# An alignment directive ahead of the first query projection of each repeating pair of an attention kernel

## The chip, the cores and the metric

The kernel runs on one core of one Trainium2 chip. The metric is the device time of one launch in microseconds, as the median of several runs. The core's engines are TensorE (PE in the profile, with its weight loads apart as PEld), VectorE (DVE), ScalarE (ACT), GpSimd (POOL) and SyncE (SP), which issues most of the DMAs. Each engine has an instruction stream of its own, which a sequencer works through in order; engines wait for each other with semaphores.

## What is computed

Cross attention of 4 x 2048 rows with 16 heads of 32 against 77 keys per batch, with an output projection, a residual and a layer norm:

```python
def reference(x, ctx_1024, mask_BxSxS2_bk1, wq, wk, wv, wo, gamma, beta):   # names shortened
    # x (4, 2048, 512), ctx_1024 (4, 77, 512); B, S, D, H = (2, 1024, 512, 16), HD = 32, EPS = 1e-05
    qs = (q @ wq).reshape(Bq, Lq, H, HD).transpose(0, 2, 1, 3)
    ks_ = (k @ wk).reshape(Bq, Lk, H, HD).transpose(0, 2, 1, 3)
    vs = (v @ wv).reshape(Bq, Lk, H, HD).transpose(0, 2, 1, 3)
    scores = jnp.einsum('bhqd,bhkd->bhqk', qs, ks_) / jnp.sqrt(jnp.float32(HD))
    scores = jnp.where(mask[:, None, :, :], -jnp.inf, scores)
    attn_w = jax.nn.softmax(scores, axis=-1)
    attn = jnp.einsum('bhqk,bhkd->bhqd', attn_w, vs)
    attn = attn.transpose(0, 2, 1, 3).reshape(Bq, Lq, H * HD)
    out = attn @ wo + q
    mu = jnp.mean(out, axis=-1, keepdims=True)
    var = jnp.mean((out - mu) ** 2, axis=-1, keepdims=True)
    return (out - mu) / jnp.sqrt(var + EPS) * gamma + beta
```

Here q is x, k and v are the context, and all of it is float32.

## The kernel before

The 8192 query rows are cut into 64 tiles of 128 rows. Two tiles make a pair, and two pairs make a group of 512 rows, for which the queries are projected together. The large projections (queries, keys, values, output) split each float32 operand into a high and a low part and add three products, high by high, high by low and low by high; scores and attention times values are plain float32, of which each matmul of the program becomes two in the instruction stream.

Three pairs of tiles and the set-up are written out at the start. After them the function `pair(n)` runs for n from 3 (`JOIN // 2`) to 26 (`CUT - 1`), and an order written out by hand (`ORDER`) ends the program. Nothing is scheduled by a planner: the order of instructions on each engine is the order of the words of the string `PAIR`, which `pair(n)` reads word for word. A word's letter names a step and its number the tile, pair or query part relative to the present one. The words that put work on TensorE are, in this order:

- `S`: the score visit, first part. `scores_pair` writes the scores of both tiles into six banks of PSUM (sc and the shared sc_e and sc_f); 96 matmuls of 32 x 64 tiles in the stream.
- `D`: `scores_rest`, the other 32 of the visit's 128.
- `O-6` and `O-5`: `o_proj`, the output projections of two earlier tiles (po), 12 matmuls each.
- `Q5` and `Q6`: `q_visit`, two query parts of a later group (pq); one has 12 matmuls, the other 13.
- `V-2`: `av`, attention times values of an earlier pair (pa), 32 matmuls in the stream.

Every matmul is preceded in the stream by a load of its weights. A matmul or a weight load carries one semaphore to wait for; where more are needed, instructions that do nothing but wait stand ahead of it. They show in the profile as EVENT_SEMAPHORE on the sequencer of the weight loads (PEldq).

The eight banks of PSUM go round (`bank`). VectorE takes the maxima of the scores out of them (`maxima`, L364) and copies the queries (`q_evac`, L209); ScalarE takes the high part of attention times values (`av_hi`, AH) and VectorE the low part (`av_lo`, L512, AL), which the output projection multiplies. So the sequencer of TensorE waits for VectorE wherever a bank is to be used again. The instruction streams themselves are fetched by DMAs on queues of their own: the profile lists 55 packets and 0.90 MB on the queue of TensorE's, 16 KB a packet, which is a block of 256 of its some 14,100 instructions.

Of the kernel before, what the change touches and what calls it, by code (L numbers as in the profile page):

```python
# [40 lines left out]
JOIN = 6  # L41
# [35 lines left out]
def xattn_layernorm(  # L77
# [15 lines left out]
    nc = tc.nc  # L93
# [198 lines left out]
    def load_mask(b):  # L292
        m8 = sb.tile([P, TPB, NK2], U8, tag="m8", bufs=1, name=f"m8_{b}")
        nc.sync.dma_start(m8, mask[b])
        mb = sb.tile([P, TPB, NK2], BF16, tag="mb", name=f"mb_{b}")
        bat[b] = (mb, m8)
# [5 lines left out]
    def mask_quarter(b, i):  # L302
        mb, m8 = bat[b]
        ts = slice(i * TPB // 4, (i + 1) * TPB // 4)
        nc.vector.tensor_tensor(mb[:, ts], m8[:, ts], mcol.to_broadcast((P, TPB // 4, NK2)), ALU.mult)
# [23 lines left out]
    def scores_pair(b):  # L329
        for t in (2 * b, 2 * b + 1):  # L330
            nmax[t] = sb.tile([P, H], F32, tag="nm", bufs=3, name=f"nm_{t}")
            sums[t] = sb.tile([P, H], F32, tag="sum", bufs=3, name=f"sum_{t}")
            scs[t] = {}
        own = [bank(f"sc_{b}_{j}") for j in range(GH)]
        both = [bank(f"sc_{b}_{j}") for j in ("e", "f")]
        units = []
        for j in range(GH):
            mine = [(2 * b, g) for g in range(NG)] + [(2 * b + 1, g) for g in range(NG)]
            for i, (t, g) in enumerate(mine):
                bk, at = (own[j], i) if i < 6 else (both[j // 2], 2 * (j % 2) + i - 6)  # L340
                scs[t][g, j] = bk[:, at * NK : (at + 1) * NK]
            units.append(mine[6:] + mine[:6] if j % 2 == 0 else mine)
        for i in range(6):
            for half in range(0, P, P // 2):
                for j in range(GH):
                    score(*units[j][i], j, half, P // 2)
        held[b] = units

    def scores_rest(b):
        units = held.pop(b)  # L350
        for i in (6, 7):
            for js in ((0, 2), (3, 1)):
                for half in range(0, P, P // 2):
                    for j in js:
                        score(*units[j][i], j, half, P // 2)
# [71 lines left out]
    def regroup(b):  # L427
        for n in range(12):
            regroup_part(b, n, nc.sync)
# [323 lines left out]
    for u in range(0, JOIN, 2):  # L753
        n = u // 2
        m, k = divmod(u, TPB)
# [123 lines left out]
    def do(op, k, part=0, queue="s"):  # L879
        if op == "k" and k >= LATE:  # L880
            scale_one(k)
        elif op == "z" and k == NT - 1:
            finish_last(k)
        elif op == "w" and k == NT - 1:
            od.pop(k)
        elif op in tile_ops:
            tile_ops[op](k)
        elif op in tile_parts:
            lo, size = (q4 * part, q4) if part < 10 else (2 * part - 20, 2) if part < 20 else (part - 20, 1)
            tile_parts[op](k, lo, lo + size)  # L890
        elif op == "s":
            (moments_one if k >= LATE else moments)(k)
        elif op in "hm":
            (recip_half if op == "h" else normalise_half)(k, part)
        elif op in visits:
            visits[op](*divmod(k, 4))
        elif op in inputs:
            inputs[op](k // 2, k % 2 * 2)
        elif op == "P":
            regroup_part(k, part, by[queue])  # L900
        elif op == "U":
            regroup_tile(k, part, by[queue])
        elif op == "R":
            flip(k, part)
        elif op == "E":
            flip_evac(k, part, nc.vector.tensor_copy if queue == "v" else nc.scalar.copy)
        elif op == "Y":
            turn_values()
        elif op == "V":
            av(k)  # L910
        elif op in "ab":
            (av_hi if op == "a" else av_lo)(k, part)
        else:
            (av_hi if op == "c" else av_lo)(k // 2, k % 2, True)

    def read(word):
        op, (k, part) = word[0], (word[1:] + ".").split(".")[:2]
        queue = part[-1:] if part[-1:].isalpha() else ""
        return op, int(k or 0), int(part[: len(part) - len(queue)] or 0), queue or "s"

    def pair(n):
        u = 2 * n
        words = PAIR.split()
        if n == JOIN // 2:
            words.remove("O-6")
            words.insert(words.index("D"), "O-6")
        for word in words:
            op, k, part, queue = read(word)
            if op == "S":
                scores_pair(n)  # L930
            elif op == "D":
                scores_rest(n)
            elif op in "LB":
                m, at = divmod(u, TPB)
                if m + 1 < NB and op == "L" and at == TPB - 10:
                    load_mask(m + 1)
                elif m + 1 < NB and op == "B" and at >= TPB - 8:
                    mask_quarter(m + 1, (at - TPB + 8) // 2)
            elif op == "P" and "." not in word:
                regroup(n + k)  # L940
            elif op in "Qq":
                if op == "Q" or divmod(2 * n + k, 4) in qp:
                    do(op, 2 * n + k)
            elif op in "gij":
                do(op, n + k)
            elif op in "PVab":
                if op in "PV" or n + k > JOIN // 2 - 3:
                    do(op, n + k, part, queue)
            elif u + k >= 0:
                do(op, u + k, part, queue)  # L950

    for n in range(JOIN // 2, CUT):
        pair(n)
# [51 lines left out]
```

## Time and profile before

| What | Value |
|---|---|
| median of 3 runs | 506.88 us (506.75 to 507.35) |
| span of the profiled execution | 505.2 us; its own time is not listed apart from the span |
| TensorE matmuls, weight loads | 496.4 us (98%), 391.0 us (77%), 6908 of each |
| VectorE, ScalarE, GpSimd | 463.3 us (92%), 472.2 us (93%), 427.0 us (85%) |
| granted TensorE clock | 0.998 of full speed |
| DMA | 109.50 MB, mean 217 GB/s |
| TensorE's share of the chain that ended last | 90% |

The page of the profile lists busy times, the chain of work that ended last (followed back from the last instruction to what released each step) and the costliest groups. In rows of instructions the first number is the start in microseconds from the span's start, the second the duration, then engine, line, operation, output<-inputs and form.

### The profile page before, as it was taken

The numbers are of one execution on the slowest core, as the hardware profiler recorded it, in microseconds if no ns is written. First come the engines' busy times: TensorE is split into PE (matmuls) and PEld (weight loads), VectorE is DVE, ScalarE is ACT, GpSimd is POOL, SyncE is SP. The second block draws the span as 40 slices with busy tenths as digits, with TensorE's granted clock in tenths as the row PEclk, the third lists the DMA queues.
The fourth block names the chain that finished last, engine by engine and source line by source line (L and its number), as shares of the span: only waits on it lengthen the run. The fifth ranks groups of instructions, "written<-read, shape, count | busy, mean of one in ns | idle before, by whom it ended". The sixth has DMA issues, their size and how long they took to land.

```text
span 505.2 us, 20438 instructions
## 1 busy us (share of the span) xinstructions
PE 496.4 (98%) x6908; PEld 391.0 (77%) x6908; DVE 463.3 (92%) x2566; ACT 472.2 (93%) x2239; POOL 427.0 (85%) x384
## 2 busy tenths in 40 slices
PE   9999999999999999999999999999999999999994
PEld 7987778777777887777788777777877777777784
DVE  6698999999989998999999988999999889999997
ACT  6798999999999999999999999999999999999861
POOL 0659368989888998988999888889988888999994
PEclk9999999999999999999999999999999999999999
DMA  8945887677778779777878878787777878667665
GB/s 308 399 165 151 207 215 194 197 191 210 213 226 227 217 211 257 188 205 227 224 218 220 237 182 248 210 228 212 228 200 204 237 214 245 171 189 209 168 210 209
DMA packets 58280, 109.50 MB, mean 217 GB/s; under 512 B 9203, under 2 KB 10739, under 8 KB 58176
## 3 DMA queue, kind: packets, MB, share of 16 engines
q1 hardware_dynamic: 55776, 103.35, 72.5%
q0 software_dynamic: 1872, 4.20, 2.7%
q8 instruction: 55, 0.90, 0.8%
q10 hardware_dynamic: 528, 0.66, 0.4%
q14 instruction: 49, 0.40, 0.2%
HBM read 41.68 MB, written 16.78 MB: 116 GB/s over the span
## 4 chain that ended last, share of the span: by engine, by line
PE 90%; ACT 4%; DVE 3%; DMA 2%; issue 1%; SPq 1%; DVEq 0%; ACTq 0%
PE pq L192 31%; PE po L557 29%; PE pa L459 11%; PE sc L321 7%; PE sc L557 3%; ACT pbuf L379 3%; PE sc_e L321 2%; PE pv L258 2%; PE pk L218 1%; PE pq L709 1%; PE pq L190 1%; DMA PT<-B 1%; PE sc_f L321 1%; DMA xtf<-xT 1%; DVE pbuf L364 1%
## 5 line engine op out<-in xcount | busy, mean ns | idle before, releaser
L379 ACT ACTIVATE pbuf<-pbuf,nm 128x77 f32<-128x77 f32 x1024 | 352.5, 349 | 8.5 <-DVE nm L364 7.5
L379 ACT ACTIVATION_READ_ACCUMULATOR pbuf<-pbuf,nm 128x1 f32 x1024 | 193.5, 189 | 0.0
L390 POOL TENSOR_TENSOR pbuf<-pbuf,ri 128x1232 f32<-128x1232 f32 x63 | 145.9, 2317 | 19.7 <-DVE ri L385 15.7
L364 DVE CUSTOM_DVE_ANT_0 pbuf<-sc,mb 128x77 f32<-128x77 f32 x828 | 144.0, 232 | 5.9 <-PE sc L321 5.6
L192 PE MATMUL pq<-xtl,wqh 128*128 128x512 f32 (+1 forms) x256 | 98.3, 384 | 0.0
L192 PE MATMUL pq<-xth,wql 128*128 128x512 f32 (+1 forms) x256 | 98.2, 384 | 0.0
L413 DVE STREAM_TRANSPOSE B<-pbuf 128x1280 f32<-128x1280 f32 x63 | 94.6, 1503 | 0.4 <-POOL pbuf L390 0.2
L557 PE MATMUL po<-woh,AH 128*128 128x512 f32 x224 | 90.6, 405 | 0.0
L192 PE MATMUL pq<-xth,wqh 128*128 128x512 f32 (+1 forms) x230 | 88.6, 385 | 0.0
L557 PE MATMUL po<-wol,AH 128*128 128x512 f32 x224 | 87.4, 390 | 0.0
L585 POOL TENSOR_TENSOR o<-o,gam 128x512 f32<-128x512 f32 x53 | 68.7, 1297 | 21.0 <-ACT o L581 21.0
L557 PE MATMUL po<-woh,AL 128*128 128x512 f32 x224 | 86.5, 390 | 0.0
L364 DVE DVE_READ_ACCUMULATOR2_ANT nm<- 128x1 f32 x1024 | 84.7, 83 | 0.0
L586 POOL TENSOR_TENSOR o<-o,bet 128x512 f32<-128x512 f32 x53 | 68.4, 1290 | 4.2
L180 POOL TENSOR_TENSOR xtl<-xtf,xth 128x1024 fp32r<-128x1024 f32 x28 | 67.5, 2412 | 0.1
L459 PE MATMUL pa<-PT,vsb 96*32 96x256 f32 x960 | 58.2, 382 | 0.7 <-DMA PT<-B 0.3
L321 PE MATMUL sc<-kct,q 32*64 32x77 f32 x3312 | 55.2, 238 | 0.5 <-DVE q L209 0.5
L192 PEld LDWEIGHTS pq<-xth,wql 128*128 128x128 f32 x256 | 48.2, 188 | 8.4
L192 PEld LDWEIGHTS pq<-xtl,wqh 128*128 128x128 f32 x256 | 48.1, 188 | 8.5
L321 PEld LDWEIGHTS sc<-kct,q 32*64 32x64 f32 x3312 | 48.7, 130 | 6.5 <-issue 4.8
L557 PEld LDWEIGHTS po<-woh,AH 128*128 128x128 f32 x224 | 42.0, 188 | 10.8 <-DVE nm L364 0.4
L192 PEld LDWEIGHTS pq<-xth,wqh 128*128 128x128 f32 x230 | 43.2, 188 | 9.0
(176 smaller groups left out, 851.6 us busy)
## 6 DMA issues: line engine op xcount, KB each, us to landing
PT<-B SPq DMA_DIRECT2D x355, 128.0 KB
xtf<-xT SPq DMA_DIRECT2D x28, 512.0 KB
o<-x SPq DMA_DIRECT2D x56, 256.0 KB
out<-o SPq DMA_DIRECT2D x56, 256.0 KB
PT<-B POOLq DMA_DIRECT2D x16, 128.0 KB, 4.5
o_end<-x SPq DMA_DIRECT2D x7, 256.0 KB
out<-o_end SPq DMA_DIRECT2D x7, 256.0 KB
xtf<-xT SPq DMA_DIRECT2D x4, 256.0 KB
```

The costliest lines, as they stand in the source:

```text
L180: nc.gpsimd.tensor_tensor(l, fx.pop((g, c)), h.bitcast(F32), ALU.subtract)
L192: nc.tensor.matmul(pq, wc, r[:, c, rs], start=(n == 0), stop=(n == 11))
L258: nc.tensor.matmul(pv, ctx_s[c][i][:, r, :], v[c], start=(n == 0), stop=(n == 11))
L321: nc.tensor.matmul(scs[t][g, j][r0 : r0 + n], qd[t // 4][q, g, at : at + n], kct[q, g, t // TPB, keys_of(j)], start=True, stop=True,)
L364: nc.vector.tensor_tensor_reduce(pb[:, i // 2, (i % 2) * NK : (i % 2 + 1) * NK], scs[t][g, j], mb[:, t % TPB, keys_of(h)], -1.0, CEIL, ALU ...
L379: nc.scalar.activation(p, p, AF.Exp, bias=nmax[t][:, i : i + 1], scale=-1.0, accum_out=sums[t][:, i : i + 1])
L390: nc.gpsimd.tensor_tensor(pv, pv, rv.to_broadcast((P, NP, 2, NK)), ALU.mult)
L413: nc.vector.transpose(bt.rearrange("p c q r -> p q c r"), pbuf[t % NPB].rearrange("p q (c r) -> p q c r", c=5),)
L459: nc.tensor.matmul(pas[b, g // 2][HD * j : HD * (j + 1), (g % 2) * BLK : (g % 2 + 1) * BLK], vsb[:, 2 * b // TPB, HD * h : HD * (h + 1)], ...
L557: nc.tensor.matmul(pos[t][:, cols], a[:, c, rs], w[:, c, cols], start=go, stop=done)
L585: nc.gpsimd.tensor_tensor(o, o, gam, ALU.mult)
L586: nc.gpsimd.tensor_tensor(o, o, bet, ALU.add)
```

## The change

In `pair(n)`, for every n over 3, a call stands ahead of the word `Q5`:

```diff
             elif op in "Qq":
+                if op == "Q" and k == 5 and n > JOIN // 2:
+
+                    nc.tensor.addr_align(256, 40)
                 if op == "Q" or divmod(2 * n + k, 4) in qp:
                     do(op, 2 * n + k)
```

`addr_align(256, 40)` is a directive and no instruction of the engine. When the program is loaded it is replaced by as many instructions without effect, from 0 to 255, as are needed for the next instruction of TensorE to land in slot 40 of a block of 256; in the form used here (no bound on their number is given) the engine's sequencer executes them all. There are 23 of these directives, in the pairs 4 to 26. With 426 instructions from one directive to the next, the score visit of the following pair starts 121 slots after slot 40, at slot 161.

On TensorE at the end of the second output projection of pair 12 (po_19, from the attention rows' parts AH and AL and the weights' parts woh and wol; pq_7_1 is the query part that `Q5` stands for there, from the rows' parts xth and xtl), this stands before:

```order
L557 MATMUL po_19_3621<-woh_69,AH_9_3495 128x512
L557 MATMUL po_19_3621<-wol_70,AH_9_3495 128x512
L557 MATMUL po_19_3621<-woh_69,AL_9_3496 128x512
L192 MATMUL pq_7_1_3651<-xth_7_3045,wqh_67 128x512 [waits DVE_49,PE_49]
L192 MATMUL pq_7_1_3651<-xtl_7_3046,wqh_67 128x512
L192 MATMUL pq_7_1_3651<-xth_7_3045,wql_68 128x512
```

And this after:

```order
L557 MATMUL po_19_3629<-woh_69,AH_9_3503 128x512
L557 MATMUL po_19_3629<-wol_70,AH_9_3503 128x512
L557 MATMUL po_19_3629<-woh_69,AL_9_3504 128x512
L944 ISA
L192 MATMUL pq_7_1_3660<-xth_7_3051,wqh_67 128x512 [waits DVE_49,PE_49]
L192 MATMUL pq_7_1_3660<-xtl_7_3052,wqh_67 128x512
L192 MATMUL pq_7_1_3660<-xth_7_3051,wql_68 128x512
```

Only the directive (L944 ISA) is new, and it stands ahead of the query part's waits; no other instruction changes its place on any engine.

## The prediction

> **What bounds the kernel now.** I read the page first: span, busy times, chain.
>
> ```profile
> span 505.2 us, 20438 instructions
> PE 496.4 (98%) x6908; PEld 391.0 (77%) x6908; DVE 463.3 (92%) x2566; ACT 472.2 (93%) x2239; POOL 427.0 (85%) x384
> PE 90%; ACT 4%; DVE 3%; DMA 2%; issue 1%; SPq 1%; DVEq 0%; ACTq 0%
> ```
>
> TensorE carries 98% of the span and 90% of the chain that ended last, so a pair costs what TensorE spends on it. The other runs' median, 506.88, lies 1.7 us above this execution's span; I work in differences from 505.2 and add them to 506.88. Next, the chain in order of time, where each repeating pair shows as one output stretch (po, 24 matmuls), one query stretch (pq: 6 and 2 and 17), one attention-times-values stretch (pa, 32) and the score visit, which the view cuts into many short pieces:
>
> ```profile
> 91.84 5.66 PE po L557 x24
> 99.10 3.88 PE pq L192 x17
> 102.98 1.86 PE pa L459 x32
> 106.47 5.67 PE po L557 x24
> 121.28 5.67 PE po L557 x24
> 135.99 5.71 PE po L557 x24
> ...
> 341.65 5.66 PE po L557 x24
> 356.47 5.69 PE po L557 x24
> ...
> 400.54 5.67 PE po L557 x24
> ```
>
> The starts of po give a pair's period: first to last here is 308.70 us over 21 periods, 14.70 each; the shortest is 91.84 to 106.47, 14.63, the longest 341.65 to 356.47, 14.82. The fixed parts do not move (po 5.66 to 5.71, pq 3.88, pa 1.86), so nearly all of the spread of up to 0.19 us lies in the score visit, between pa and po. That is the whole prize: if each of the 23 pairs took the shortest period, 23 x 0.07 = 1.6 us.
>
> **What the change takes and adds.** A pair is 426 TensorE instructions: 24 + 25 + 32 + 128 matmuls, a weight load with each, and eight waits that stand alone (two at L192, four at L459, two at L321; rows below). Three pairs are 1278, two short of five blocks of 256, so today the block edge meets the score visit in three places in turn, shifting by only two slots every third pair. With the directive a pair must fill whole blocks: 512, so 512 - 426 = 86 padding instructions per pair, and the first query event sits at slot 40, the first score weight load 121 later, at 161. Nothing else is added, and no matmul, wait or DMA changes place; POOL's and SP's queues are not passed.
>
> *The padding's place.* It stands after the second output projection and ahead of the wait for the first query bank. What I must know is how long TensorE's sequencer is idle there, and how far it runs ahead of the array. One pair, from the windows of VectorE, of the weight loads and of L192, L459 and L321:
>
> ```profile
> 195.08 0.69 DVE L512 TENSOR_TENSOR AL<-pa,AH 128x512 fp32r<-128x512 f32 x1
> 198.21 0.24 DVE L364 CUSTOM_DVE_ANT_0 pbuf<-sc,mb 128x77 f32<-128x77 f32 x1
> 199.82 0.19 PEld L557 LDWEIGHTS po<-woh,AL 128*128 128x128 f32 x1
> 200.05 0.19 PEld L192 LDWEIGHTS pq<-xth,wqh 128*128 128x128 f32 x1
> L192 PEldq EVENT_SEMAPHORE  x2: 51/51/51, 198.5 to 200.2; - x2
> L459 PEldq EVENT_SEMAPHORE  x4: 51/51/51, 201.8 to 202.1; - x4
> L321 PEldq EVENT_SEMAPHORE  x2: 51/51/51, 191.7 to 191.9; - x2
> ```
>
> The ninth output matmul waits for the low half of the attention rows (AL), done at 195.08 + 0.69 = 195.77. After it nothing is left to wait for until the query event, which starts at 198.5, right after the VectorE maximum that frees its bank (198.21 + 0.24 = 198.45). So the sequencer stands at that event while the array still works off output matmuls, and the array wants the first query weights at 200.05. The 32 instructions in between cost little: the two L321 events, with 12 weight loads and matmuls between them, are 0.2 us apart, so I put 0.3 us. Window one, free of any effect: 198.45 - 195.77 - 0.3 = 2.4 us, or 28 ns for each of 86. Window two, until the array starves: 200.05 - 195.77 - 0.3, less 0.25 for the event and for the dispatch of the load, 3.7 us, or 43 ns each.
>
> *The price of one padding instruction* is in no row. Rows to bound it:
>
> ```profile
> 178.27 0.13 PEld L321 LDWEIGHTS sc_f<-kct,q 32*64 32x64 f32 x1
> 178.27 0.13 PEld L321 LDWEIGHTS sc<-kct,q 32*64 32x64 f32 x1
> 178.28 0.13 PEld L321 LDWEIGHTS sc_e<-kct,q 32*64 32x64 f32 x1
> 178.29 0.13 PEld L321 LDWEIGHTS sc<-kct,q 32*64 32x64 f32 x1
> ...
> 0.24 0.10 POOL L996 MEMSET const-float32-0.0<- 128x1 f32 x1 [0.24 <-issue]
> 0.27 0.10 POOL L996 MEMSET const-float32-1.0<- 128x1 f32 x1
> 0.30 0.10 POOL L996 MEMSET const-bfloat16-1.0<- 128x1 bf16 x1
> 0.33 0.10 POOL L996 MEMSET const-uint8-127<- 128x1 uint8 x1
> ```
>
> Below: weight loads of a score visit start some 7 ns apart, so 86 x 7 = 0.6 us. Above: the four L459 events follow each other by 0.3 / 3 = 0.1 us, so 86 x 0.1 = 8.6 us. In the middle: GpSimd's sequencer starts four small fills 30 ns apart, ordinary instructions without a wait. Padding has no semaphore either, and it isn't a matmul that goes straight to the array, so the fills are its nearest row: 86 x 30 = 2.6 us, 0.2 over window one and 1.1 inside window two. The query event then passes 0.2 us later, with the array still fed. I cost the padding at 0; its cover is the output projection's 24 matmuls, and if that cover ends (over 43 ns), the query projection is late next, once per pair.
>
> The Trainium skill, "DMA: Bandwidth & Descriptors", section "Anatomy of one DMA", puts an engine sequencer's dispatch at about 50 ns. By it the padding would be an estimated 4.3 us, 0.6 over the second window, and the 23 pairs would cost some 14 us. No row here shows a padding instruction, so it is not excluded.
>
> *The first padding* isn't 86: it depends on what the loader puts ahead of the program, which the trace doesn't show, and is 0 to 255. At 30 ns the middle, 128, is 3.8 us, 0.1 over the window; the worst is 7.7, so 4.0 once. I take +0.2.
>
> *The block edge.* Does its place matter? Sort the periods by their number in the sequence of three: by the 22 starts whose first and last rows stand above, the three groups average 14.67, 14.70 and 14.72 us. Scatter within a group (14.63 to 14.72, 14.63 to 14.81, 14.65 to 14.82) is larger than the distance between them. If every pair took the best group's mean, 23 x 0.03 = 0.7 us; if the worst's, a loss of 0.5. Counted from the program's first instruction the best group's visits begin near slot 155, close to the new 161; but the loader's own instructions ahead of the program shift that count by an unknown number, so 161 may fall to any group. I take 0.4 us of gain.
>
> *More blocks.* The page has the instruction fetch of TensorE on its own queue:
>
> ```profile
> q8 instruction: 55, 0.90, 0.8%
> ```
>
> 0.90 MB in 55 packets is 16 KB, 256 instructions of 64 B, each. The 22 later paddings add 22 x 86 / 256 = 7.4 blocks, with the first some 8: 63 packets, 0.1% more of the DMA engines. Hidden behind the 0.8% that is hidden today.
>
> The Trainium skill, "Runtime: NRT & Kernel Launch", section "Instruction fetch mechanics", speaks against the change: crossing a 16 KiB boundary is mostly hidden. By it the block-edge term is 0 and the sum +0.2. The trace agrees so far as the three groups differ by no more than 0.05 us.
>
> Sum: padding 0, first padding +0.2, block edge -0.4, fetch 0: -0.2, so 506.88 - 0.2 = 506.7.
>
> **Rivals.** (1) *Slower: padding at the price of an event on TensorE's queue.* It decides above 43 ns. An event is recorded as 51 ns: 86 x 51 = 4.4 us, 0.7 beyond the window, 23 x 0.7 = 16 us, 523. At 0.1 us a piece: 8.6 - 3.7 = 4.9, 113 us, 620. For it: the padding runs on the same sequencer as those events, whose follow-on time is more than three times that of GpSimd's fills. Against it: an event handles a semaphore, padding doesn't. The page's 50 ns, named above from the Trainium skill, leads into this rival. (2) *Faster: the block edge is what stretches the score visit, and 161 is a good place for it.* Then all pairs go to between the shortest period and the best group's mean, -0.7 to -1.6 us, 505.3 to 506.2; over 1.0 it can be measured. For it: two of the three groups are longer. Against: the scatter within them; a VectorE wait in the visit explains it as well. (3) *No change at all, or a change that isn't what it says:* if the loader adds nothing, or the edge has no price and padding none: 506.9, and the fetch packets tell which (55 or 63).
>
> **How the numbers follow.** A measurement of this kernel can tell about 0.2%, 1.0 us, from no change. Padding hidden and the edge worth less than 1.0 us, my forecast together with rival 3: 0.38, its own range 505.9 to 507.9. Rival 2 in its measurable part: 0.27, down to 505.2. Rival 1: 0.35, of which about half lies below 530 (53 ns, 10 ns over the limit: 86 x 10 x 23 = 20 us, and 3 for the first padding). So faster 0.27, same 0.38, slower 0.35, and the range 505.2 to 530 leaves out some 0.18, nearly all above.
>
> **What would show it.** Hidden: the first query weight load still follows the last output one by 0.23 us (199.82 to 200.05), the query event starts at most some 0.3 us later than the VectorE maximum before it, and periods stay at 14.63 to 14.82. Not hidden: an idle stretch of the weight loads ahead of L192 in every pair, put down to "issue". Edge right: periods all alike and near 14.65; edge worthless: as scattered as now. Fetch: 62 to 64 packets on the instruction queue. Wrong altogether: a padding price over 43 ns.

## The result, and the profile after

| | before | after |
|---|---|---|
| median of the runs on one chip | 507.1 us (506.4 to 507.6, 6 runs) | 588.06 us (582.72 to 591.47, 6 runs) |
| span of the profiled execution | 505.2 us | 586.8 us |
| granted TensorE clock | 0.998 | 0.964 |

The changed kernel is slower: the ratio to before is 1.158, with a 95% interval of 1.154 to 1.161. Every ratio, here and below, leaves out executions over 1.5% longer than the shortest of the same kernel (one of the six here, four of the six of e8, single ones of e1, e2 and e7), while the medians count them. The page, with the rows that answer to those of before (the last one is the fetch of TensorE's instructions):

```profile
span 586.8 us, 22437 instructions
PE 517.7 (88%) x6908; PEld 400.7 (68%) x6908; DVE 465.8 (79%) x2566; ACT 473.5 (81%) x2239; POOL 427.9 (73%) x384
PE 47%; DVE 44%; ACT 3%; issue 2%; DMA 2%; SPq 1%; DVEq 0%; ACTq 0%
q8 instruction: 63, 1.03, 0.8%
```

The span grew by 81.6 us while the work of VectorE, ScalarE and GpSimd stayed where it was (DVE 463.3 before, 465.8 now). There are 1999 instructions more, which the trace shows as 107 in the first padding and 22 x 86. TensorE's share of the chain fell from 90% to 47%, and VectorE's rose to 44%. That last row misleads, as the groups and the waits show. From the page's groups, the same line of before first, then of after, and then the waits of the weight loads after (total, times, longest):

```profile
L192 PE MATMUL pq<-xth,wqh 128*128 128x512 f32 (+1 forms) x230 | 88.6, 385 | 0.0
```

```profile
L192 PE MATMUL pq<-xth,wqh 128*128 128x512 f32 (+1 forms) x230 | 95.6, 416 | 59.4 <-DVE nm L364 52.0
```

```profile
PEld pq L192 <- issue: 68.5, 23, 4.3
```

The first query matmul of a pair now finds the array idle, 59.4 us in all where there was none. The group puts most of it to VectorE's maximum (nm L364), the last semaphore that the query event handles. The weight load in front of the same matmul, however, waits 68.5 us for "issue", 23 times, once per directive: nothing that the profile shows held it. That is TensorE's own sequencer, busy. One pair in the order of the instructions (the last output weight load, the padding of this pair in one row with its first and last start, the query events, the first query weight load):

```profile
212.52 0.19 PEld L557 LDWEIGHTS po<-woh,AL 128*128 128x128 f32 x1
215.48 0.19 PEld L192 LDWEIGHTS pq<-xth,wqh 128*128 128x128 f32 x1 [2.78 <-issue]
```

```profile
L944 PEldq NOP  x86: 13/13/13, 208.9 to 215.3; - x86
L192 PEldq EVENT_SEMAPHORE  x2: 51/51/51, 215.4 to 215.6; - x2
```

The 86 instructions without effect appear as NOP, each recorded as 13 ns, but their starts run from 208.9 to 215.3: 6.4 / 85 = 75 ns from one to the next. The sequencer reaches them while the array is still in the output projection, 0.45 us after VectorE has finished the low half of the attention rows (at 208.46 in this pair, and within 5 ns of that delay in all 22 later pairs), and it is done 2.78 us after the last output weight load has ended. Before, the query load followed the output load by 0.23 us.

The clock adds to it. The chain in order of time, for the same pair and the one ahead of it, and then three windows around the query stretch of this pair (busy times of PE, PEld, DVE, ACT and POOL, the granted clock, the DMA's share and GB/s):

```profile
198.23 1.62 PE pq L192 x6
200.09 3.88 PE pq L192 x17
...
215.51 1.65 PE pq L192 x6
217.59 5.25 PE pq L192 x17
```

```profile
213.50:217.00 3.50, 1.49 (x7) 1.26 (x8) 3.43 (x22) 3.50 (x22) 2.06 (x1) 1.00 0.58 164
217.00:220.40 3.40, 3.40 (x11) 2.72 (x10) 0.69 (x3) 2.76 (x13) 2.00 (x6) 0.50 0.89 204
220.40:224.00 3.60, 3.60 (x35) 2.49 (x37) 2.30 (x4) 0.10 (x1) 3.52 (x3) 1.00 0.86 226
```

In the pair at 198 the query stretch runs at the full clock and takes as long as before (3.88 for its 17). In the pair at 215 the granted clock is 0.50 from 217.0 to 220.4, and the stretch takes (217.59 - 215.51) - (200.09 - 198.23) + (5.25 - 3.88) = 1.6 us longer. The trace has 11 such stretches of 3.41 us among the pairs; before had none there.

Which pairs these are can be read from the trace. The starts of the stretches (87.27, 124.82, 141.88, 162.36, 216.98 us and so on) lie whole multiples of 3.413 us apart: 11, 5, 6 and 16 for these. If the time of the pairs is cut into windows of this length on that grid, the array was busy, by the profile, for at most 43% of each of the 11 windows right before a stretch at half clock, and for at least 45% of each of the 100 other windows at full clock. In e8 below, 7 such windows and 105 others lie on the same two sides. So in this kernel a pair is slowed down when most of its idle time falls into one window of the grid; where it is spread over two, the clock stays. The window before the stretch at 216.98 (busy 1.47 of 3.41 us), and one that none followed (1.55):

```profile
213.57:216.98 3.41, 1.47 (x7) 1.24 (x8) 3.34 (x22) 3.41 (x22) 2.04 (x1) 1.00 0.59 165
104.34:107.75 3.41, 1.55 (x7) 1.32 (x8) 3.38 (x20) 3.41 (x21) 2.17 (x1) 1.00 0.66 183
```

So the loss divides like this. From the starts of the matmuls, the 23 steps from the last output matmul to the first query matmul take 68.4 us together, against 5.2 before: the waits cost the array 63.1 us. The 11 query stretches with half clock in them are 1.6 us longer each than those of before (5.57 us), 18 us. Together 81 of the 81.6.

### The profile page after: what moved, and what is told of

Same layout as the page of the kernel before. It is cut to its first block, busy times and chain, and to the rows that moved or that the text cites. A ratio compares the mean times of both kernels' runs of the same rounds, so it can differ in the third digit from the quotient of the medians.

```text
span 586.8 us, 22437 instructions
## 1 busy us (share of the span) xinstructions
PE 517.7 (88%) x6908; PEld 400.7 (68%) x6908; DVE 465.8 (79%) x2566; ACT 473.5 (81%) x2239; POOL 427.9 (73%) x384
## 4 chain that ended last, share of the span: by engine, by line
PE 47%; DVE 44%; ACT 3%; issue 2%; DMA 2%; SPq 1%; DVEq 0%; ACTq 0%
PE pq L192 28%; DVE pbuf L364 19%; PE pa L459 8%; DVE B L413 7%; DVE AL L512 6%; DVE o L560 5%; ACT pbuf L379 3%; PE sc L557 2%; DVE nm L364 2%; PE sc L321 2%; PE pv L258 1%; PE pq L190 1%; PE pk L218 1%; PE sc_e L321 1%; PE pq L709 1%
## 5 line engine op out<-in xcount | busy, mean ns | idle before, releaser
L379 ACT ACTIVATION_READ_ACCUMULATOR pbuf<-pbuf,nm 128x1 f32 x1024 | 197.7, 193 | 0.0
L390 POOL TENSOR_TENSOR pbuf<-pbuf,ri 128x1232 f32<-128x1232 f32 x63 | 144.3, 2291 | 68.4 <-DVE ri L385 64.2
L364 DVE CUSTOM_DVE_ANT_0 pbuf<-sc,mb 128x77 f32<-128x77 f32 x828 | 143.9, 232 | 6.4 <-PE sc L321 6.1
L192 PE MATMUL pq<-xth,wqh 128*128 128x512 f32 (+1 forms) x230 | 95.6, 416 | 59.4 <-DVE nm L364 52.0
L192 PE MATMUL pq<-xth,wql 128*128 128x512 f32 (+1 forms) x256 | 104.7, 409 | 0.0
L192 PE MATMUL pq<-xtl,wqh 128*128 128x512 f32 (+1 forms) x256 | 104.6, 409 | 0.0
L508 ACT CAST AH<-pa 128x512 fp32r<-128x512 f32 x60 | 34.5, 583 | 81.8 <-PE pa L459 81.8
L192 PEld LDWEIGHTS pq<-xth,wqh 128*128 128x128 f32 x230 | 46.1, 201 | 77.8 <-issue 68.5
L209 DVE COPY q<-pq 128x512 f32<-128x512 f32 x60 | 40.7, 686 | 61.0 <-PE pq L192 60.9
L364 DVE DVE_READ_ACCUMULATOR2_ANT nm<- 128x1 f32 x1024 | 85.0, 83 | 0.0
L459 PE MATMUL pa<-PT,vsb 96*32 96x256 f32 x960 | 58.2, 382 | 1.3 <-PE pq L192 0.5
L192 PEld LDWEIGHTS pq<-xth,wql 128*128 128x128 f32 x256 | 52.0, 203 | 9.7
L192 PEld LDWEIGHTS pq<-xtl,wqh 128*128 128x128 f32 x256 | 52.4, 205 | 8.6
```

Of the source, the lines that this page charges most:

```text
L192: nc.tensor.matmul(pq, wc, r[:, c, rs], start=(n == 0), stop=(n == 11))
L209: nc.vector.tensor_copy(qd[g][:, m, :], pq)
L364: nc.vector.tensor_tensor_reduce(pb[:, i // 2, (i % 2) * NK : (i % 2 + 1) * NK], scs[t][g, j], mb[:, t % TPB, keys_of(h)], -1.0, CEIL, ALU ...
L379: nc.scalar.activation(p, p, AF.Exp, bias=nmax[t][:, i : i + 1], scale=-1.0, accum_out=sums[t][:, i : i + 1])
L390: nc.gpsimd.tensor_tensor(pv, pv, rv.to_broadcast((P, NP, 2, NK)), ALU.mult)
L459: nc.tensor.matmul(pas[b, g // 2][HD * j : HD * (j + 1), (g % 2) * BLK : (g % 2 + 1) * BLK], vsb[:, 2 * b // TPB, HD * h : HD * (h + 1)], ...
```

## The experiments

The theory after the result, A: each padding instruction holds TensorE's sequencer for some 71 to 75 ns, and what exceeds the sequencer's lead over the array is lost. The rival, B: it is the alignment or the block edges that lose the time, and the padding only stands there. Ratios below are to runs of the kernel before on the same chip (507.1 to 507.4 us).

**e1: same alignment, padding not executed.** The directive's third number bounds how many padding instructions are executed; above it the sequencer jumps over them.

```diff
-                    nc.tensor.addr_align(256, 40)
+                    nc.tensor.addr_align(256, 40, 0)
```

> The same directive, slot 40 of 256, but with at most 0 padding instructions executed: the loader puts a jump at the head of the padding. Slots, blocks and fetches are as in the changed kernel, only the executing of the padding is gone. Theory A (each padding instruction takes TensorE's sequencer 71 to 76 ns, and what goes over the cover of the output projection is lost): the whole loss goes, 506 to 508 us, and what is left beside 507.1 is the worth of the block edge's place (505.3 if slot 161 is a good place, 507.5 if a bad one) and one jump per pair, hidden. Theory B (longer stream, 8 more blocks to fetch, the block edge in a bad place): the loss stays, 580 to 590 us.

Measured: 508.49 us, ratio 1.002 (1.001 to 1.003), half a microsecond over theory A's range. The source line of the directive now has jumps and no NOP:

```profile
L944 PEldq COMPARE_BRANCH  x23: 727/1247/1507, 79.4 to 403.1; - x23
```

The slots are the same as in the changed kernel, and 63 instruction blocks are fetched here as well. Nearly all of the loss is gone, so B is out: alignment and jumps together cost 0.4 to 1.3 us by the interval. A jump is recorded as 0.7 to 1.5 us, yet the query weights are not late. In one pair the jump runs from 211.8 to 213.3, and the query event starts at 214.1, right after the VectorE maximum that ends at 214.00: the sequencer would have waited for the query's bank in that time anyway.

**e2, e3, e4: fewer padding instructions.** A directive with a smaller block pads less; several of them with falling offsets pad by a fixed number in every pair: 38, 54 and 70. (Each loop is put on one line here.)

```diff
-                    nc.tensor.addr_align(256, 40)
+                    for off in (0, 15, 14): nc.tensor.addr_align(16, off)          # e2: 38 a pair
+                    nc.tensor.addr_align(32, 0); nc.tensor.addr_align(32, 31)      # e3: 54
+                    for off in (0, 15, 14, 13, 12): nc.tensor.addr_align(16, off)  # e4: 70
```

> 38 padding instructions per pair in place of 86, by directives of 16 slots in a chain; the stream is 464 slots a pair and the block edge moves from pair to pair. Theory A: padding starts 1.52 us after the output projection, 38 x 0.0755 = 2.9 us, done 0.9 us before the query weights are wanted: no loss, 506.5 to 508 us. Theory B (loss by slots): 38 of 86 of the 81 us, about 543 us.

> 54 padding instructions per pair, by two directives of 32 slots. Theory A: 54 x 0.0755 = 4.08 us from 1.52 us on, and 0.13 for the event: 5.73 us against 5.35 before, 0.3 to 0.4 us late per pair, 23 pairs: 7 to 9 us, 514 to 516 us, TensorE's clock at full speed. Theory B: 54 of 86 of 81 us, 558 us.

> 70 padding instructions per pair, by a chain of five directives of 16 slots. Theory A: 70 x 0.0755 = 5.3 us, 1.5 to 1.6 us late per pair, 35 to 37 us: 542 to 544 us, if the clock stays at full speed with the array idle about 1.8 us a pair; with half-speed stretches of 3.4 us as in the changed kernel (1.6 us each, in half of the pairs) 560 us. Theory B: 573 us.

Measured: 510.46 us (ratio 1.006, 1.005 to 1.007) with 38; 514.02 (1.013, 1.012 to 1.014) with 54, which theory A gave; 540.56 (1.066, 1.065 to 1.067) with 70, 1.4 under its range. The waits of the query weights with 54 and then with 70:

```profile
PEld pq L192 <- issue: 6.4, 20, 0.4
```

```profile
PEld pq L192 <- issue: 33.6, 22, 1.9
```

From 54 to 70 there are 16 more in each of 22 pairs, and the time rises by 26.5 us: 75 ns each. Part of that is another thing, as two score visits of the run with 70 lost 1.2 and 1.0 us; the output stretches alone, counted up to the first query matmul, grow from 5.77 to 6.89 us, 70 ns each. With 54 the limit is just passed (0.3 us a pair), with 70 each pair but the first loses 1.2 to 1.7 us on the array; in neither does the clock fall (0.997 and 0.996). With 38 no query load is late, and the expectation of 506.5 to 508 is missed for another reason. One output stretch of its profiled execution is 0.7 us longer than the rest, and one score visit, which began at 193.8, 2.5 us (its weight loads):

```profile
197.72 0.13 PEld L321 LDWEIGHTS sc_f<-kct,q 32*64 32x64 f32 x1 [2.33 <-issue]
```

By the count of slots this is the block's edge: here the edge shifts from pair to pair, and it lay 249 slots into this visit. The packet with the next block started at 194.92 and took 1.36 us, and the stream went on 1.44 us after its end. Block edges do cost something, then, when the block is late.

**e8: same padding, no block edge among it.** In the changed kernel the edge lies behind the 46th padding instruction, and in 11 of the 22 later pairs the sequencer pauses there by 0.2 to 1.2 us, 3.5 us in all. Moved by 70 slots, the 86 lie in one block.

```diff
-                    nc.tensor.addr_align(256, 40)
+                    nc.tensor.addr_align(256, 110)
```

> As the changed kernel, with padding that is executed, but its place 70 slots later, so that all 86 padding instructions of a pair lie within one block and no block edge among them. Theory A (each padding instruction takes TensorE's sequencer some 71 to 75 ns, which is the loss): 86 x 71 to 75 = 6.1 to 6.5 us, so the query weights come 2.4 to 2.9 us late in each pair, 560 to 588 us depending on how many stretches at half clock follow the idle time; the gaps after the 46th padding instruction (0.2 to 1.2 us in some ten pairs of the changed kernel) are gone. Rival B (the edge inside the padding, that is the late fetch of a block, makes the loss): the loss goes with the edge, 506 to 512 us.

Measured: ratio 1.148 (1.143 to 1.153), which is 582 us and rests on two of six executions. The six range from 579.83 to 613.75 us, with a median of 592.81, and the granted clock goes from 0.984 in the shortest to 0.956 in the longest; so how often the clock was halved is part of the scatter. The profiled execution is one of 592.65 us. In one pair of it, the padding and the query weights:

```profile
L944 PEldq NOP  x86: 13/13/13, 198.9 to 205.2; - x86
```

```profile
205.37 0.19 PEld L192 LDWEIGHTS pq<-xth,wqh 128*128 128x128 f32 x1 [2.67 <-issue]
```

6.3 / 85 = 74 ns, and 2.67 us of idle time in place of 2.78. The pauses behind the 46th are gone; the loss stays. The edge inside the padding was worth some 3.5 us of the 81. The total can't be compared that closely: the first padding has 177 instructions here, against 107, and three pairs wait 4.0 us instead of 2.7, after a pause in the output stretch ahead of the padding.

**e10: same padding in two places.** 50 instructions ahead of the query event, and 36 ahead of the four events of attention times values (L459); the first padding alone is jumped over.

```diff
-                    nc.tensor.addr_align(256, 40)
+                    nc.tensor.addr_align(256, 60, 100)
...
             elif op in "PVab":
+                if op == "V" and n > JOIN // 2:
+                    nc.tensor.addr_align(256, 148)
```

> The same 86 padding instructions of a pair are executed, but in two parts: 50 ahead of the query event, and 36 ahead of the four events of the attention-times-values stretch (L459), by a second directive; the score visit begins at slot 217 as in e9_jump96, and the 127 instructions of the first padding alone are jumped over. Theory A (the price is 71 to 75 ns of TensorE's sequencer for each, and only what exceeds the sequencer's lead at that place is lost: 50 x 75 = 3.8 against 3.7 us, 36 x 75 = 2.7 against about 3.5 us between those events at 202.1 and the array's first attention matmul at 205.6): no idle time over 0.2 us ahead of L192 or of L459, 505.9 to 509 us. Rival G (executed padding costs the array a fixed time wherever it stands, or starves whatever comes behind it): 2.5 us per pair as in the changed kernel, 560 to 588 us; a part of that, if the second place has no lead to spare: 36 x 75 = 2.7 us per pair at most, up to 566 us.

Measured: 509.27 us, ratio 1.004 (1.002 to 1.006), just over theory A's range. The rows of the two directives, and the waits of the query weights:

```profile
L944 PEldq NOP  x1100: 13/13/13, 94.8 to 409.2; - x184
```

```profile
L951 PEldq NOP  x828: 13/13/13, 85.7 to 413.7; - x166
```

```profile
PEld pq L192 <- issue: 2.0, 6, 0.4
PEld pq L192 <- PE po L557: 1.6, 3, 0.6
```

1928 padding instructions are executed, against 1999 in the changed kernel, and 79 of its 81 us are gone. This decides for A in its second half too: a padding instruction has no price of its own for the array. The sequencer has a lead of nearly 4 us at the first place and of at least 2.7 us (36 x 75 ns) at the second, and 86 at one place overdraw it, where 50 and 36 at two places hardly do: L192 waits 3.6 us in all and up to 0.6 at a time, where theory A allowed 0.2, and the loads of L459 in the pairs wait at most 0.4 us, as before.

**e5, e6, e7, e9: the place of the block edge.** With the padding jumped over, only the place remains. C: an edge early in the score visit costs nothing, later it stretches the visit; D: the place is without effect. The directive of e1 with other offsets:

```diff
-                    nc.tensor.addr_align(256, 40)
+                    nc.tensor.addr_align(256, 110, 0)    # e5: edge 25 slots into the visit
+                    nc.tensor.addr_align(256, 126, 0)    # e6: 9 slots
+                    nc.tensor.addr_align(256, 210, 0)    # e7: 181 slots
+                    nc.tensor.addr_align(256, 96, 0)     # e9: 39 slots
```

> The padding is jumped over as in e1_jump40, and the first query event stands at slot 110 instead of 40, so the score visit begins at slot 231 and the block edge lies 25 slots into it, where the visits of before and of the runs so far took 1.62 to 1.63 us. Theory C (an edge early in the visit, while TensorE's sequencer is still far ahead of the array, costs nothing; later it stretches the visit by 0.06 to 0.1 us): nearly all visits at 1.62 to 1.64 us, a period of 14.63 to 14.66, 505.4 to 506.4 us beside 507.2 for the kernel before. Rival D (the place of the edge is without effect, and VectorE's waits scatter the visits): visits scatter from 1.62 to 1.82 as before, 507.0 to 508.7 us, as e1_jump40.

> As e5_jump110, with the query event at slot 126: the score visit begins at slot 247 and the edge lies 9 slots into it. Theory C: as e5_jump110, 505.4 to 506.5 us, unless the next block is not there yet so near the visit's start. Rival D: 507.0 to 508.7 us.

> As e5_jump110, with the query event at slot 210: the score visit begins at slot 75 and the edge lies 181 slots into it, late. Theory C: visits of 1.69 to 1.79 us in most pairs, a period of 14.71 to 14.79, 507.8 to 509.6 us. Rival D: 507.0 to 508.7 us, with visits that scatter from 1.62 to 1.82 as in e5_jump110.

> The padding is jumped over, with the query event at slot 96: the score visit begins at slot 217, its block edge lies 39 slots in, and the next edge 37 slots into the output projection instead of 23 (e5_jump110) or 7 (e6_jump126). Theory E (an edge early in the visit spares the visit 0.06 us, but a 256-instruction visit uses its block up in 1.6 us, so the block behind it can come late, and the output stretch pays for that unless its edge lies behind enough queued matmuls: 37 slots in, some 18 matmuls of 0.23 us cover it): visits mostly at 1.62 to 1.70 us, output stretches at 5.57 to 5.62 us in every pair, 505.9 to 506.6 us beside 507.1 for before. Rival F (late blocks come anywhere, whatever the place): one to three output stretches or visits longer by 0.5 to 2.5 us, 506.8 to 509 us.

Measured, with the visits (from a visit's first score matmul to the first output matmul) and the output stretches (to the first query matmul) of 21 pairs of one profiled execution each, worked out from the starts of the matmuls:

| | edge in the visit | visit, mean us | visits up to 1.65 us | output stretch, mean, longest us | median us | ratio |
|---|---|---|---|---|---|---|
| before | three places in turn | 1.686 | 7 | 5.585, 5.62 | 507.1 | |
| e6 | 9 | 1.638 | 16 | 5.889, 6.20 | 513.39 | 1.011 (1.009 to 1.013) |
| e5 | 25 | 1.648 | 15 | 5.635, 6.17 | 507.05 | 1.000 (0.999 to 1.002) |
| e9 | 39 | 1.677 | 11 | 5.581, 5.61 | 506.97 | 0.999 (0.997 to 1.000) |
| e1 | 95 | 1.706 | 4 | 5.583, 5.61 | 508.49 | 1.002 (1.001 to 1.003) |
| e7 | 181 | 1.734 | 3 | 5.581, 5.62 | 512.40 | 1.013 (1.008 to 1.018) |

The visits follow C, and their mean grows with the edge's place from 1.638 to 1.734 us; D would have them alike. Visits with the edge in one place still differ among themselves (1.62 to 1.84 us in e7), so the place is not all of it. The times do not follow: I expected e5 and e6 at 505.4 to 506.5, e7 at 507.8 to 509.6 and e9, by theory E, at 505.9 to 506.6, and all four came out above (e5 and e9 within the ranges of their rivals D and F). With an early edge the next one comes 256 slots on, early in the output projection, and there its block is late. The weight loads of e5 at such a place, which lies 24 instructions or 12 loads into the stretch:

```profile
301.31 0.19 PEld L557 LDWEIGHTS po<-woh,AL 128*128 128x128 f32 x1
302.21 0.19 PEld L557 LDWEIGHTS po<-woh,AH 128*128 128x128 f32 x1 [0.71 <-PE po L557]
```

Its packet started at 299.45, 2.24 us after the start of the visit where others start some 0.2 us after it, took 1.36 us, and the stream went on 1.4 us later. In e5 this stretched two of 21 output stretches by 0.6 us, in e6, with the edge 7 slots in, 17 by 0.1 us or more. In e9, with some 18 queued matmuls ahead of it, none. e9 is 0.45 us under the kernel before on the same chip (507.42), which an interval that reaches to 1.000 doesn't tell from nothing. For e7 the visits explain 21 x 0.05 = 1 us of its 5; its profiled execution lost some 3 more behind the last pair, with a stretch of 3.41 us at half clock at 455 among it, and I do not know why. Why a few packets start 1.5 to 2 us later than the others stays open as well. No version here is shown to beat the kernel before.

## Why the prediction was wrong

**The step that failed** is the price of one padding instruction. The prediction bounded it by 7 and 100 ns and took 30, because GpSimd's fills were "its nearest row"; so it put the padding's cost at 0, where it was 63 us of waits. The changed kernel shows 71 ns from one to the next in the median and 75 in the mean (the pauses at the block edge left out), since about every 16th takes longer; e3 and e4 give 70 to 75 from the count. The nearest row in size was on the same sequencer: the L459 events, 0.1 us apart. Here the row of another engine's sequencer did not carry over, nor did the duration recorded (13 ns here, 51 for the events), which is only a part of it.

**The windows held.** The sequencer was put 0.3 us after the low half of the attention rows (AL) is done; it reaches the padding 0.45 us after that, in every one of the 22 later pairs. So the reading of what holds the sequencer was right. The second window was put at 3.7 us, 43 ns each; it is 6.5 - 2.5 = 4.0 us (86 x 75 ns, and 2.5 us of it lost on the array), 46 each. With 75 for 30 the prediction's own sum gives 86 x (75 - 43) = 2.8 us for each of 22 pairs and 107 x 75 ns - 3.7 = 4.3 us for the first, 65 us; the waits cost 63.

**Rival 1 is what happened**, with its place, its limit and its sign, and its two prices (51 and 100 ns) lie on both sides of the measured one. The Trainium skill, "DMA: Bandwidth & Descriptors", section "Anatomy of one DMA", names about 50 ns for the sequencer's dispatch, but as a part of the fixed cost of one DMA and not of an instruction without effect. The trace shows 71 to 75 ns for these, so the page's figure led to the right side, to 14 us in place of 81.

**A term was missing**: the clock. An array that idles for 2.5 us or more in each pair fell to half clock in 11 of 23 pairs, 18 us in all, and the sum of the prediction had no place for it. The Trainium skill, "TensorE: Matmul & The Clock Gate", Part 1, tells of a free-running window of 3413 ns and half the clock after at least one idle window. The trace agrees with the window: the stretches are 3.41 us long and start on a grid of 3.413 us. But the window ahead of a stretch need not be idle throughout: it was up to 43% busy here. In e4, with 1.2 to 1.7 us of idle time in a pair, no window of the pairs was under 64% busy, and the clock never fell. The limit of 43 to 45% is none for other work: e7's one stretch, behind its last pair, followed a window that was 62% busy by the profile.

**The first padding** was put at 0.2 us, with 4.0 as its worst. It is 107 instructions, 8.0 us, and the wait of 4.3 us is the longest of the waits row; right in its kind, and mis-sized by the same price.

**The block edge** was taken as a gain of 0.4 us. The three groups of periods were more than scatter. Counted with the loader's instructions, by the first padding of 107, the edge of the best group lies 32 to 44 slots into the visit, and of the others 118 to 130 and 202 to 214; their visits in the kernel before take 1.648, 1.691 and 1.716 us in the mean, which follows the place as those of e5 to e9 do. So rival 2's mechanism has some truth. But the prediction's best group began near slot 155 only without the loader's instructions, as it said, and slot 161 puts the edge at 95, a poor place: with the padding jumped over the change costs 0.2%. In the changed kernel itself all the later visits take 1.62 us, with the edge at 95 too. With the pair 2.5 us longer both the sequencer and VectorE have more time there, so this doesn't separate the edge from the waits for VectorE, and how much of the spread is VectorE's stays open.

**The fetch** was right in its count, 63 packets with a forecast of 62 to 64, but not quite hidden: the pauses at the edge inside the padding add up to 3.5 us. The Trainium skill, "Runtime: NRT & Kernel Launch", section "Instruction fetch mechanics", has block crossings mostly hidden. The trace agrees for most edges here, but not for every one in or right behind a stretch that uses up 256 instructions in 1.6 us: 0.6 us were lost at one in e5, 2.3 at one in e2.

## What to carry to other kernels

Price an instruction without effect by the pitch of its own engine's sequencer, from start to start in the trace, not by its recorded duration, and compare the sum with the lead that the sequencer has at that place: here some 4 us or 50 instructions were free or nearly so, and each one beyond cost some 75 ns in every pair. If a stream has to be aligned, jump over the padding, or spread it over several places where the sequencer waits anyway. And where a matmul is said to wait for another engine, look at its weight load as well: "issue" there meant TensorE's own sequencer in this kernel.

## What the runs showed of the hardware

- A NOP on TensorE's queue held its sequencer for 71 ns and is recorded as 13; 86 in a row averaged 75.
- Idle times of 2.5 us or more on the array in each pair brought stretches of 3.41 us at half clock in 11 of 23 pairs; of 1.2 to 1.7 us, none. The stretches started on a fixed grid of 3.413 us, and each in the pairs followed a window of it in which the array was at most 43% busy.
- A jump over padding that crosses a block's edge is recorded as 0.7 to 1.5 us (all 23 of e1, and the first of e5, e6 and e9), one within a block as 0.17 to 0.29 us (the others of these, and e7's). With a lead of some 4 us neither made the query weights late.
- An instruction block of 16 KB took 0.9 to 2.1 us as a packet, and after a late one the stream resumed 1.2 to 1.6 us behind the packet's end (16 pauses in e2, e4, e5 and e6). A score visit uses up 256 instructions in 1.62 us, so it is the stretch around it where an edge was felt.
